# Dividing the first layer's attention sums on VectorE in 32 by 32 pieces instead of through TensorE

## The chip, the cores and the metric

The kernel runs on one core of one Trainium2 chip. The metric is the device time in microseconds of that core; the time of a kernel is the median of several runs. The five engines are written as in the profile: PE is TensorE's matmul, PEld its weight load, DVE is VectorE, ACT is ScalarE, POOL is GpSimd, and SP issues DMAs. All data are float32.

## The reference

Two transformer layers act on x of shape (4, 512, 256), each with gated cross attention to a context of the same shape and a gated feed-forward part. What matters here is the first layer's attention and what surrounds it:

```python
Q = heads(layernorm(x) @ Wq.T + bq)         # 16 heads of 16
K = heads(ctx @ Wk.T + bk)
V = heads(ctx @ Wv.T + bv)
scores = einsum('bhqd,bhkd->bhqk', Q, K) / 4 - 0.1 * |q - k|
attn = softmax(scores)
out = einsum('bhqk,bhkd->bhqd', attn, V)     # back to (b, 512, 256)
x = x + tanh(g_xattn[0]) * (out @ Wo.T + bo)
# feed-forward part of layer 0: weights rounded to -1, 0, 1
x = x + tanh(g_ffn[0]) * (relu(layernorm(x) @ W1q.T + b1) @ W2q.T + b2)
# layer 1: attention with relu on q, k, v and no output matrix, added to x;
# then a mixture of four experts, one per token, with a layernorm behind it
```

## The kernel before, in words

**Groups and slots.** The 16 heads of one batch element are worked in four groups of four heads, (tt, e) with tt = 0, 1 and e = 0, 1; there are 32 groups, 16 for each layer, and group s of layer 0 belongs to batch element s // 4. A group needs four units, one for each block of 128 keys. The main loop goes over these units: `for u in range(-NT, n_units)` (line 1019), 128 of them. One turn of it is called a slot in what follows. In every slot `scores(u, ...)` (line 525) puts out two rounds of matmuls that fill the array by rows of 32: half of a round are the scores whose maxima DVE takes (`maxima`, pm, for unit u + 6), the other half are the scores that ACT turns into exponentials (`weights`, psc, for unit u). DVE drains a slot's four pm banks at line 502, ACT its four psc banks at line 517, and in layer 0 POOL multiplies a part of p by a decay table (line 520).

**What a slot adds.** After the scores `slot(u)` (line 964) emits the rest of that turn. In slots with u % 4 == 0 it is `weighted` (line 538), 32 matmuls that sum a group's weights times values into `po`, which ACT copies to `oT` (line 551). In slots with u % 4 == 2 it is `turned` (line 553): four PE transposes of the maxima (`pmT`) and, for the group before, four PE transposes of oT (`pn`), a reciprocal of the column that holds the sum of weights (`rec`, line 571) and a product (`o`, line 577). After that come jobs from chains: norms, projections of keys and queries (`project`, line 440), values, the feed-forward parts (`ffn0`, line 587), the rounding of the two weight matrices (`quantize`, line 264), and the routing of layer 1.

**What sets their order.** The order on PE, DVE, ACT and POOL is the order in which the program emits instructions; the Tile framework adds the waits. A chain is a list of steps (job, cost, delay), with a first unit, a last unit and chains that must be done before. A slot counts what it has used and takes the job with the earliest due unit among those that may start:

```python
(job, cost, _), last = c["steps"][0]
if last <= u or cost == 0 or used + cost / 2 < SLOT:      # SLOT = 3.1
    can.append((last, len(can), c))
```

`weighted` counts 3.5, `turned` 1.0, and the others what their step says (1.75 for four full matmuls' worth of work).

**Buffers.** All PSUM tiles come from one pool of eight banks that are given out in turn, so each new bank waits until the one given out eight before has been read. xT (input of a projection or of the feed-forward part, transposed) has three places; o has two, oT two, and q four.

**The feed-forward part of layer 0.** `ffn0(b)` begins with `turn_o` (line 591): POOL adds the output bias to x, PE transposes o with eight transposes (`pt_o`) and ACT copies them to `oTT`. Two `product` jobs multiply by Wo; then follow a norm, its transposes, eight `hidden` jobs (`ph`) and two `output` jobs (`py_f`), the first use of the second weight matrix `w2q`. The rounding of a matrix takes a sum, thresholds, four passes `under` on POOL (line 291) and four passes `over` on DVE (line 298).

Of the kernel before, what the change touches and what calls it, by code (L numbers as in the profile page):

```python
# [11 lines left out]
F32 = mybir.dt.float32  # L12
U32 = mybir.dt.uint32
AF = mybir.ActivationFunctionType
ALU = mybir.AluOpType
# [4 lines left out]
P = 128  # L20
B, S, D = 4, 512, 256
H, DK = 16, 16
NT = S // P
# [21 lines left out]
def flamingo_kernel(ctx: ExitStack, tc: tile.TileContext, t: dict, out: bass.AP):  # L45
# [11 lines left out]
    def bank_psum(name):  # L57
        return ps.tile([P, 512], F32, tag="bank", name=name)
# [303 lines left out]
    def transposed(src, dst, name, alone=False):  # L362

        for c in range(NC):
            pt = bank_psum(f"pt_{name}{c}")
            for n in range(NT):
                nc.tensor.transpose(pt[:, ts(n, P)], src[:, n, ts(c, P)], ident)
            (nc.scalar.copy if alone or c == 0 else nc.vector.tensor_copy)(dst[:, c, :], pt)
# [18 lines left out]
    def prepare(layer, b, eng=None, meanwhile=None):  # L387

        nm = f"a{layer}_{b}"
        st = {}  # L390

        def stats():
            st["xn"] = act.tile([P, NT, D], F32, tag="xn", name=f"xn_{nm}")
            first, st["more"], st["rows"] = layernorm(
                x[b], st["xn"], 1e-5, nm, eng, meanwhile
            )
            first()

        def more_stats():
            st["more"]()  # L400

        def norm():
            st["rows"]()

        def turn():
            xTs[layer, b] = act.tile([P, NC, S], F32, tag="xT", name=f"xT_{nm}", bufs=3)
            transposed(st["xn"], xTs[layer, b], nm, layer == 0 and b > 0)

        def values(n0):
            def run():  # L410
                wv = attn_w[layer]["wv"]
                vh = v_sb[b % 2][1]
                pv = bank_psum(f"pv{nm}{n0}")
                for n in range(2):
                    for c in range(NC):
                        nc.tensor.matmul(  # L416
                            pv[:, ts(n, D)], lhsT=cT[b][:, c, ts(n0 + n, P)], rhs=wv[:, c, :],
                            start=(c == 0), stop=(c == NC - 1),
                        )
                if layer == 0:  # L420
                    nc.scalar.copy(
                        vh[:, n0 : n0 + 2, :, 0:DK], pv.rearrange("p (n h d) -> p n h d", n=2, d=DK)
                    )
# [15 lines left out]

    def project(layer, b, tt):  # L440

        nm = f"{layer}_{b}{tt}"

        def product(w, src, name):
            pp = bank_psum(f"{name}{nm}")
            for c in range(NC):
                nc.tensor.matmul(  # L447
                    pp, lhsT=attn_w[layer][w][:, c, ts(tt, P)], rhs=src[:, c, :],
                    start=(c == 0), stop=(c == NC - 1),
                )  # L450
# [12 lines left out]

        def keys(between=None, halves=range(2)):
            pk = product("wk", cT[b], "pk")
            if between:
                between()
            for e in halves:
                key_half(pk, e)

        def queries():
            pq = product("wq", xTs[layer, b], "pq")
            for e in range(2):
                q = act.tile([P, S], F32, tag="q", name=f"q{nm}{e}", bufs=4)
                h = half[:, e : e + 1]
                if layer == 0:
                    nc.scalar.activation(q, pq, AF.Identity, bias=bqk[:, 0, tt, e : e + 1], scale=h)
                elif e == 0:
                    nc.scalar.activation(q, pq, AF.Relu, scale=h)
                else:  # L480
                    nc.vector.tensor_scalar(q, pq, h, 0.0, ALU.mult, ALU.max)
                qs[layer, b, tt, e] = q

        return [(keys, 1.75, 1), (queries, 1.75, 0)]
# [65 lines left out]
        pos[s] = act.tile([P, S], F32, tag="oT", name=f"oT{s}")  # L550
        nc.scalar.copy(pos[s], po)  # L551

    def turned(shifted, divided):


        if shifted is not None:
            g = groups[shifted]
            m = m_sb[g[0]][g[3]]
            pm = bank_psum(f"pmT{shifted}")
            for n in range(NT):  # L560
                nc.tensor.transpose(pm[:, ts(n, P)], m[:, n].rearrange("p h w -> p (h w)"), ident)  # L561
            q2s[g] = act.tile([P, S], F32, tag="q2", name=f"q2_{shifted}")
            nc.vector.tensor_tensor(q2s[g], qs[g], pm, ALU.subtract)
        if divided is not None:
            layer, b, tt, e = groups[divided]
            pn = bank_psum(f"pn{divided}")
            for n in range(NT):
                nc.tensor.transpose(pn[:, ts(n, P)], pos[divided][:, ts(n, P)], ident)  # L568
            pn = pn.rearrange("p (n h w) -> p n h w", h=HG, w=HP)
            rec = sml.tile([P, NT, HG], F32, tag="rec", name=f"rec{divided}")  # L570
            nc.vector.reciprocal(rec, pn[:, :, :, DK])
            if layer == 1:
                nc.vector.tensor_scalar_mul(rec, rec, gx1)
            if (tt, e) == (0, 0):
                os_[layer, b] = act.tile([P, NT, D], F32, tag="o", name=f"o{layer}_{b}")
            ov = os_[layer, b].rearrange("p n (t i e d) -> p n t i e d", t=NC, i=HG, e=2)
            nc.vector.tensor_tensor(  # L577
                ov[:, :, tt, :, e, :], pn[:, :, :, 0:DK],
                rec.unsqueeze(3).to_broadcast([P, NT, HG, DK]), ALU.mult,
            )  # L580
            if layer == 1:
                eng = nc.vector if b >= B - 2 and (tt, e) == (1, 1) else nc.gpsimd
                xv = x[b].rearrange("p n (t i e d) -> p n t i e d", t=NC, i=HG, e=2)[:, :, tt, :, e, :]
                eng.tensor_tensor(xv, xv, ov[:, :, tt, :, e, :], ALU.add)  # L584


    def ffn0(b):

        st = {}

        def turn_o():
            st["oT"] = act.tile([P, NC, S], F32, tag="xT", name=f"oTT{b}", bufs=3)
            nc.gpsimd.tensor_tensor(
                x[b], x[b], bo0.unsqueeze(1).to_broadcast([P, NT, D]), ALU.add
            )
            transposed(os_[0, b], st["oT"], f"o{b}", True)

        def product(n0):
            return lambda: residual(
# [15 lines left out]
            )  # L615

        def turn():
            st["xT"] = act.tile([P, NC, S], F32, tag="xT", name=f"xTf0_{b}", bufs=3)
            transposed(st["xn"], st["xT"], f"f0_{b}")

        def hidden(f):
# [15 lines left out]
        def output(n2):  # L637
# [3 lines left out]

        return (
            [
                (turn_o, 0.9, 0), (product(0), 1.75, 1), (product(2), 1.75, 0), (stats, 0, 1),
                (more_stats, 0, 1),
            ],
            [
# [17 lines left out]
    def route(b, eng=None):  # L665
# [20 lines left out]
            nc.sync.dma_start(out=rd[:, :, D : 2 * D], in_=x[b])  # L686

        def turn():
            st["xT"] = act.tile([P, NC, S], F32, tag="xT", name=f"xTf1_{b}", bufs=3)
            transposed(st["xn"], st["xT"], f"f1_{b}")  # L690

        def products():
# [250 lines left out]
    (totals2, *_), *quant2 = quantize(w2f, "w2")  # L943
    totals = {0: (totals1, 0), 1: (totals1, 2), 2: (totals2, 0), 3: (totals2, 2)}
    quant = chain(quant1, 4, 17)
    chain(quant2, 12, 29, quant)
    chain([(bias_columns, 0, 0), (output_bias, 0.9, 2)], 4, 14)
    fetches = [
        (lambda j=j, f=f: f(j), 0, 0)
# [14 lines left out]
    def slot(u):  # L964
# [3 lines left out]
            used += 3.5  # L968
        if u % NT == 2 and u > 0:
            s = u // NT  # L970
            turned(s + 1 if s + 1 < len(groups) else None, s - 1 if s > 0 else None)
            used += 1.0
        while True:
            can = []
            for c in chains:
# [42 lines left out]
    key_rows(1, 1, nc.gpsimd)  # L1018
    for u in range(-NT, n_units):
        if u == 0:  # L1020
            turned(0, None)
            early_values()
            other_constants()
        if u == 4:
# [85 lines left out]
    hidden_tile(0)  # L1110
    weighted(last)
    turn_tile(1)
    turned(None, last)
    att.__exit__(None, None, None)
    act = ctx.enter_context(tc.tile_pool(name="moe", bufs=2))
    fetch_weights(2)
# [110 lines left out]
```

## Time and profile before

| What | Value |
|---|---|
| Median of 3 runs | 869.88 us (869.17 to 870.01) |
| The profiled execution, its own time | 868.27 us |
| Its span, first to last instruction | 866.0 us |
| Mean granted clock of TensorE | 0.987 |
| PE busy | 836.0 us, 97% of the span |
| DVE busy | 539.2 us, 62% |
| ACT busy | 422.9 us, 49% |
| POOL busy | 271.8 us, 31% |

The slots run from about 15 us to 704 us of the span; the experts of layer 1 take the rest. Slot 16, the first that the change touches, begins at 101.7 us, slot 57 at 328.7 us and slot 101 at 587.7 us. Busy times are sums over an engine's instructions; matmuls are pipelined, and their ends are modelled, so that PE's share counts waits that lie under a running matmul. A group's row gives the line, the engine, the operation, what it writes and reads with the shapes, how often, the busy time, the mean of one in ns, and behind the last bar the engine's idle time before it and who ended that. In a timeline's row the first number is the start, the second the length of the merged run, and in square brackets stands the idle time before it with its releaser.

### The profile page before, as it was taken

The page shows a single profiled execution, that of the slowest core. Times are in us where ns is not written, and L with a number is a line of the kernel's source. Part 1 is how long each engine was busy: PE and PEld are TensorE (multiplying, and loading weights), DVE is VectorE, ACT ScalarE, POOL GpSimd, SP SyncE. Part 2 cuts the span into 40 slices and gives each one's busy share as a digit, 9 for nine tenths or more (in the row PEclk, how much of TensorE's full clock was granted, in tenths as well). Part 3 has the DMA queues.
Part 4 walks back from the last instruction along what each step waited for, and adds up shares of the span by engine and source line. Part 5 has one row for each costly group of instructions (what it writes and reads, how often), then busy time and mean ns, then how long its engine had stood idle before and what let it go on. Part 6 is the DMA issues. An engine that isn't in the chain of part 4 may idle for free.

```text
span 866.0 us, 13669 instructions
## 1 busy us (share of the span) xinstructions
PE 836.0 (97%) x5294; PEld 475.1 (55%) x5294; DVE 539.2 (62%) x1170; ACT 422.9 (49%) x886; POOL 271.8 (31%) x435
## 2 busy tenths in 40 slices
PE   6999999999999999999999999999999999999995
PEld 3444454445464445545446444554444448999994
DVE  6778777665745675467663776567677715644443
ACT  2475565553545563546543664346466563233331
POOL 5536465324242343302100220003002034445542
PEclk9999999999999999999999999999999999999998
DMA  9100000000000000000000010001001046456650
GB/s 314 59 1 1 1 1 2 1 1 1 1 13 25 1 1 1 1 26 1 1 1 1 25 50 1 1 1 50 2 1 48 1 147 215 162 183 201 196 190 15
DMA packets 17776, 42.03 MB, mean 49 GB/s; under 512 B 2158, under 2 KB 12144, under 8 KB 15280
## 3 DMA queue, kind: packets, MB, share of 16 engines
q0 software_dynamic: 5168, 27.08, 9.5%
q1 hardware_dynamic: 12128, 13.54, 4.6%
q8 instruction: 42, 0.69, 0.3%
q10 hardware_dynamic: 416, 0.54, 0.2%
q14 instruction: 22, 0.18, 0.1%
HBM read 34.86 MB, written 6.68 MB: 48 GB/s over the span
## 4 chain that ended last, share of the span: by engine, by line
PE 76%; DVE 7%; issue 6%; POOL 4%; DMA 4%; ACT 2%; POOLq 0%; ACTq 0%; DVEq 0%
PE pm L488 15%; PE po L545 13%; PE psc L488 13%; PE py_f L375 6%; PE ph L625 6%; PE pk L447 4%; PE pva L416 3%; PE pq L447 3%; DVE m L502 3%; DMA out_dram<-y,put 3%; PE pmT L561 2%; PE py_wo L375 2%; PE pn L568 2%; POOL wg L894 2%; POOL out_dram L1102 1%
## 5 line engine op out<-in xcount | busy, mean ns | idle before, releaser
L502 DVE TENSOR_REDUCE m<-pm 128x1 f32<-128x512 f32 x512 | 316.6, 681 | 133.3 <-PE psc L488 130.7
L517 ACT ACTIVATE p<-psc 128x512 f32<-128x512 f32 x512 | 267.2, 603 | 158.0 <-PE psc L488 156.0
L488 PE MATMUL psc<-q,k 32*128 32x512 f32 x1024 | 284.9, 631 | 2.1 <-DVE m L502 1.9
L488 PE MATMUL pm<-k,q 32*128 32x512 f32 x1024 | 266.4, 619 | 2.9 <-DVE m L502 2.0
L520 POOL TENSOR_TENSOR p<-p,dec 128x256 f32<-128x256 f32 x128 | 93.3, 732 | 184.1 <-ACT p L517 184.1
L488 PEld LDWEIGHTS pm<-k,q 32*128 32x128 f32 x1024 | 95.1, 185 | 86.5 <-issue 59.7
L488 PEld LDWEIGHTS psc<-q,k 32*128 32x128 f32 x1024 | 108.6, 185 | 55.8 <-issue 26.5
L545 PE MATMUL po<-p,v 128*32 128x512 f32 x1024 | 117.9, 601 | 1.7 <-DVE m L502 1.6
L1065 ACT ACTIVATE ha<-pg,wg 128x128 f32<-128x128 f32 x152 | 43.2, 369 | 88.6 <-PE pg L1059 83.3
L545 PEld LDWEIGHTS po<-p,v 128*32 128x32 f32 x1024 | 31.6, 110 | 84.5 <-issue 63.3
L1059 PE MATMUL pg<-xs,wg 128*128 128x128 f32 x608 | 71.2, 275 | 0.8 <-DVE xn_f L356 0.8
L1059 PEld LDWEIGHTS pg<-xs,wg 128*128 128x128 f32 x608 | 70.5, 192 | 2.8 <-POOL rstd_f L336 1.2
L1075 PE MATMUL pyf<-wo,ha 128*128 128x256 f32 x304 | 68.6, 379 | 0.0
L584 POOL TENSOR_TENSOR x<-x,o 128x256 f32<-128x256 f32 x14 | 10.2, 730 | 174.0 <-DVE o L577 142.1
L625 PE MATMUL ph<-xTf,w1q 128*128 128x512 f32 x128 | 60.2, 603 | 0.0
L1075 PEld LDWEIGHTS pyf<-wo,ha 128*128 128x128 f32 x304 | 56.4, 190 | 6.9
L551 ACT COPY oT<-po 128x512 f32<-128x512 f32 x32 | 18.7, 585 | 81.4 <-PE po L545 81.4
L375 PE MATMUL py_f<-w2q,h 128*128 128x256 f32 x256 | 57.0, 381 | 0.0
L375 PEld LDWEIGHTS py_f<-w2q,h 128*128 128x128 f32 x256 | 48.0, 190 | 9.2 <-DVE m L502 3.0
L447 PE MATMUL pk<-cT,wk 128*128 128x512 f32 x68 | 35.2, 642 | 7.5 <-DMA cT<-in_ctxT_dram 7.4
L1079 DVE TENSOR_TENSOR y<-y,pyf 128x256 f32<-128x256 f32 x19 | 8.0, 421 | 53.2 <-PE pyf L1075 52.9
L625 PEld LDWEIGHTS ph<-xTf,w1q 128*128 128x128 f32 x128 | 22.4, 190 | 27.7 <-issue 17.2
(197 smaller groups left out, 800.4 us busy)
## 6 DMA issues: line engine op xcount, KB each, us to landing
x<-in_x_dram SPq DMA_DIRECT2D x4, 512.0 KB, 8.6
rows_d<-xn_f SPq DMA_DIRECT2D x4, 512.0 KB, 3.8
rows_d<-x SPq DMA_DIRECT2D x4, 512.0 KB, 3.8
cT<-in_ctxT_dram SPq DMA_DIRECT2D x3, 512.0 KB, 9.5
w1q<-in_w_dram SPq DMA_DIRECT2D x1, 1024.0 KB, 9.1
w2q<-in_w_dram SPq DMA_DIRECT2D x1, 1024.0 KB, 11.3
wo<-in_wo_dram SPq DMA_DIRECT2D x2, 512.0 KB, 3.8
rows<-in_rows_dram SPq DMA_DIRECT2D x1, 640.0 KB, 9.3
```

Of the source, the lines that this page charges most:

```text
L375: nc.tensor.matmul(py[:, n, :], lhsT=operand(c, n0 + n), rhs=w[:, c, :], start=(c == 0), stop=(c == chunks - 1),)
L416: nc.tensor.matmul(pv[:, ts(n, D)], lhsT=cT[b][:, c, ts(n0 + n, P)], rhs=wv[:, c, :], start=(c == 0), stop=(c == NC - 1),)
L447: nc.tensor.matmul(pp, lhsT=attn_w[layer][w][:, c, ts(tt, P)], rhs=src[:, c, :], start=(c == 0), stop=(c == NC - 1),)
L488: nc.tensor.matmul(out_, lhsT=lhs[r, ts(n, P)], rhs=rhs[r, :], start=True, stop=True)
L502: nc.vector.tensor_reduce(m[:, n, 2 * pair + i, r : r + 1], pm[i], AX.X, ALU.max)
L517: nc.scalar.activation(p[:, i, :], psc[i], AF.Exp, scale=SCALE)
L520: nc.gpsimd.tensor_tensor(d, d, dec.unsqueeze(1).to_broadcast([P, 2, P]), ALU.mult)
L545: nc.tensor.matmul(po[i * HP : (i + 1) * HP, :], lhsT=v_sb[b % 2][0][:, kt, c0 : c0 + HP], rhs=ps_exp[NT * s + kt, i // 2][:, i % 2, :], s ...
L625: nc.tensor.matmul(ph, lhsT=w1q[:, c, ts(f, P)], rhs=st["xT"][:, c, :], start=(c == 0), stop=(c == NC - 1),)
L1059: nc.tensor.matmul(ph[:, f, :], lhsT=w[:, c, ts(f2 * NF // 2 + f, P)], rhs=xs[j][:, c, :], start=(c == 0), stop=(c == NC - 1),)
L1065: nc.scalar.activation(ha[:, f, :], ph[:, f, :], AF.Gelu, bias=wg[j][:, NC * FF + fa : NC * FF + fa + 1],)
L1075: nc.tensor.matmul(py, lhsT=hs[j, f // 4][:, f % 4, :], rhs=wo1[f // 4][:, f % 4, :], start=(f == 0), stop=(f == NF - 1),)
```

## The change

`turned` is divided in two functions, `shifted` (the transposes of the maxima, as before) and `divided` (the division as before, for layer 1 and for batch element 0 of layer 0). For batch elements 1 to 3 of layer 0 `divided_blocks` takes its place: DVE transposes oT in 32 by 32 pieces, takes the reciprocals and the products in that layout, and after the second group of a pair transposes both together back, in pieces, straight into the layout that Wo's matmul reads. It is emitted in slots u % 4 == 0, two groups behind, after `weighted`. `turn_o` then has nothing to do for these batch elements, and its bias add is a step of its own. The second half of q in layer 0 is read out of PSUM by DVE for b = 2 and 3. The second matrix's rounding starts at unit 17 (was 12) and is due at 33 (was 29). xT has two places instead of three, and the transposed input of the routing uses the place of `blocks`.

```diff
-            xTs[layer, b] = act.tile([P, NC, S], F32, tag="xT", name=f"xT_{nm}", bufs=3)
+            xTs[layer, b] = act.tile([P, NC, S], F32, tag="xT", name=f"xT_{nm}", bufs=2)
...
-                if layer == 0:
+                if layer == 0 and (e == 0 or b < 2):
                     nc.scalar.activation(q, pq, AF.Identity, bias=bqk[:, 0, tt, e : e + 1], scale=h)
+                elif layer == 0:
+                    nc.vector.tensor_scalar(q, pq, h, bqk[:, 0, tt, e : e + 1], ALU.mult, ALU.add)
...
+    def by_blocks(s):
+        return groups[s][0] == 0 and groups[s][1] > 0
+
+    TB = S // HP
+
+    def divided_blocks(s):
+        layer, b, tt, e = groups[s]
+        if e == 0:
+            blocks[b, tt] = act.tile([P, 2, TB, HP], F32, tag="blocks", name=f"blocks{s}", bufs=1)
+        turn, both = (blocks[b, tt][:, i] for i in range(2))
+        nc.vector.transpose(turn.rearrange("p a w -> p (a w)"), pos[s])
+        rec = sml.tile([P, TB], F32, tag="rec", name=f"rec{s}")
+        nc.vector.reciprocal(rec, turn[:, :, DK])
+        if (tt, e) == (0, 0):
+            os_[layer, b] = act.tile([P, NC, S], F32, tag="o", name=f"o{layer}_{b}")
+        nc.vector.tensor_tensor(
+            both[:, :, e * DK : (e + 1) * DK], turn[:, :, 0:DK],
+            rec.unsqueeze(2).to_broadcast([P, TB, DK]), ALU.mult,
+        )
+        if e == 1:
+            nc.vector.transpose(os_[layer, b][:, tt, :], both.rearrange("p a w -> p (a w)"))
...
-        def turn_o():
-            st["oT"] = act.tile([P, NC, S], F32, tag="xT", name=f"oTT{b}", bufs=3)
+        def output_biases():
             nc.gpsimd.tensor_tensor(
                 x[b], x[b], bo0.unsqueeze(1).to_broadcast([P, NT, D]), ALU.add
             )
-            transposed(os_[0, b], st["oT"], f"o{b}", True)
+
+        def turn_o():
+            st["oT"] = os_[0, b]
+            if b == 0:
+                st["oT"] = act.tile([P, NC, S], F32, tag="xT", name=f"oTT{b}", bufs=2)
+                transposed(os_[0, b], st["oT"], f"o{b}", True)
...
-                (turn_o, 0.9, 0), (product(0), 1.75, 1), (product(2), 1.75, 0), (stats, 0, 1),
+                (output_biases, 0, 0), (turn_o, 0 if b else 0.9, 0), (product(0), 1.75, 1 + int(b > 0)),
+                (product(2), 1.75, 0), (stats, 0, 1),
...
-            st["xT"] = act.tile([P, NC, S], F32, tag="xT", name=f"xTf1_{b}", bufs=3)
+            st["xT"] = act.tile([P, NC, S], F32, tag="blocks", name=f"xTf1_{b}", bufs=1)
...
-    chain(quant2, 12, 29, quant)
+    chain(quant2, 17, 33, quant)
...
-            turned(s + 1 if s + 1 < len(groups) else None, s - 1 if s > 0 else None)
-            used += 1.0
+            if s + 1 < len(groups):
+                shifted(s + 1)
+                used += 0.5
+            if s > 0 and not by_blocks(s - 1):
+                divided(s - 1)
+                used += 0.5
+        if u % NT == 0 and u >= 2 * NT and by_blocks(u // NT - 2):
+            divided_blocks(u // NT - 2)
```

More of the change, by code (lines that the diff above doesn't have):

```diff
@@ L551, in weighted @@
         nc.scalar.copy(pos[s], po)
[L553 to L584, printed above, removed]
@@ new lines, in shifted @@
+    def shifted(s):
+        g = groups[s]
+        m = m_sb[g[0]][g[3]]
+        pm = bank_psum(f"pmT{s}")
+        for n in range(NT):
+            nc.tensor.transpose(pm[:, ts(n, P)], m[:, n].rearrange("p h w -> p (h w)"), ident)
+        q2s[g] = act.tile([P, S], F32, tag="q2", name=f"q2_{s}")
+        nc.vector.tensor_tensor(q2s[g], qs[g], pm, ALU.subtract)
+    def by_blocks(s):
[17 more added lines that the diff above has]
+            nc.vector.transpose(os_[layer, b][:, tt, :], both.rearrange("p a w -> p (a w)"))
@@ new lines, in flamingo_kernel, with divided @@
+    blocks = {}
+    def divided(s):
+        layer, b, tt, e = groups[s]
+        pn = bank_psum(f"pn{s}")
+        for n in range(NT):
+            nc.tensor.transpose(pn[:, ts(n, P)], pos[s][:, ts(n, P)], ident)
+        pn = pn.rearrange("p (n h w) -> p n h w", h=HG, w=HP)
+        rec = sml.tile([P, NT, HG], F32, tag="rec", name=f"rec{s}")
+        nc.vector.reciprocal(rec, pn[:, :, :, DK])
+        if layer == 1:
+            nc.vector.tensor_scalar_mul(rec, rec, gx1)
+        if (tt, e) == (0, 0):
+            os_[layer, b] = act.tile([P, NT, D], F32, tag="o", name=f"o{layer}_{b}")
+        ov = os_[layer, b].rearrange("p n (t i e d) -> p n t i e d", t=NC, i=HG, e=2)
+        ov = ov[:, :, tt, :, e, :]
+        nc.vector.tensor_tensor(
+            ov, pn[:, :, :, 0:DK], rec.unsqueeze(3).to_broadcast([P, NT, HG, DK]), ALU.mult
+        )
+        if layer == 0:
+            return
+        eng = nc.vector if b >= B - 2 and (tt, e) == (1, 1) else nc.gpsimd
+        xv = x[b].rearrange("p n (t i e d) -> p n t i e d", t=NC, i=HG, e=2)[:, :, tt, :, e, :]
+        eng.tensor_tensor(xv, xv, ov, ALU.add)
@@ L617, in turn @@
         def turn():
-            st["xT"] = act.tile([P, NC, S], F32, tag="xT", name=f"xTf0_{b}", bufs=3)
+            st["xT"] = act.tile([P, NC, S], F32, tag="xT", name=f"xTf0_{b}", bufs=2)
             transposed(st["xn"], st["xT"], f"f0_{b}")
@@ L1020, in flamingo_kernel @@
         if u == 0:
-            turned(0, None)
+            shifted(0)
             early_values()
@@ L1112, in flamingo_kernel @@
     turn_tile(1)
-    turned(None, last)
+    divided(last)
     att.__exit__(None, None, None)
```

## The prediction

> **What bounds the kernel now.** I read the page first (busy shares, then the slices), then the groups of instructions kept apart by shape, then the timeline slot by slot, then the list of waits. "Slot" is one turn u of the main loop: two rounds of scores on PE, then the jobs that `slot(u)` adds; in the timeline it begins where pm and psc start again after other PE work.
>
> The page: the span, the engines, and the slices of PE and DVE.
> ```profile
> span 866.0 us, 13669 instructions
> ...
> PE 836.0 (97%) x5294; PEld 475.1 (55%) x5294; DVE 539.2 (62%) x1170; ACT 422.9 (49%) x886; POOL 271.8 (31%) x435
> ...
> PE   6999999999999999999999999999999999999995
> ...
> DVE  6778777665745675467663776567677715644443
> ```
> PE is full in nearly every slice; DVE, which takes the work over, is at five to seven tenths. But a busy PE may be a PE that waits on a buffer, so the slots must be read one by one.
>
> Three stretches in the view by windows: PE's slot 38 (one product after pmT and pn), slot 44 (the 32 matmuls of `weighted`), slot 99 (scores alone). Columns: length, then busy time and count of PE, PEld, DVE, ACT, POOL.
> ```profile
> 222.70:227.52 4.82, 4.82 (x34) 3.06 (x33) 3.68 (x8) 2.93 (x6) 2.17 (x3) 1.00 0.00 0
> ...
> 257.92:263.49 5.57, 5.57 (x50) 1.94 (x49) 3.17 (x5) 2.90 (x6) 3.22 (x5) 1.00 0.21 49
> ...
> 578.03:580.68 2.65, 2.12 (x17) 0.84 (x16) 2.37 (x8) 1.73 (x4) 0.73 (x1) 1.00 0.00 0
> ```
> With jobs in it a slot is as long as PE's work: 5.57 us full, 4.82 us with one product. Without jobs (2.65 us) it is as long as DVE's four maxima, 2.48 us. So work taken off PE is worth its time only where the slot keeps enough other PE work.
>
> **The change, part by part.** The groups by shape that I cost with:
> ```profile
> L502 DVE TENSOR_REDUCE m<-pm 128x1 f32<-128x512 f32 x512 | 316.6, 681 | 133.3 <-PE psc L488 130.7 <-PE pm L488 2.6
> ...
> L568 PE MATMUL pn<-ident,oT 128*128 128x128 f32 x128 | 20.6, 284 | 0.3 <-ACT oT L551 0.3
> ...
> L577 DVE TENSOR_TENSOR o<-pn,rec 128x256 f32<-128x256 f32 x32 | 13.6, 424 | 1.1
> ...
> L571 DVE RECIPROCAL rec<-pn 128x16 f32<-128x16 f32 x32 | 7.9, 248 | 8.7 <-PE pn L568 8.7
> ...
> L368 DVE COPY xTf<-pt_f 128x512 f32<-128x512 f32 x8 | 5.5, 683 | 1.2 <-PE pt_f L367 1.2
> ...
> L367 PE MATMUL pt_o<-ident,o 128*128 128x128 f32 x32 | 4.5, 281 | 0.5 <-DVE m L502 0.5
> ```
> (1) The pn transposes of groups 4 to 15 go. Their means (284 ns) overlap; the cost on PE is the pitch, read in slot 38:
> ```profile
> 224.67 0.66 PE L561 MATMUL pmT<-ident,m 128*128 128x128 f32 x4
> 225.20 0.66 PE L568 MATMUL pn<-ident,oT 128*128 128x128 f32 x4
> 225.70 1.89 PE L375 MATMUL py_wo<-wo,oTT 128*128 128x256 f32 x8
> ```
> From pn's start to the product's is 0.50 us. The product inherits the PSUM bank that pn had, and that was free at 225.20, so it can start there: 12 x 0.50 = -6.0 us, in slots 22, 26, ... 66.
>
> (2) The eight transposes of `turn_o` go for b = 1 to 3, slots 35, 51, 67. In slot 51 pt_o starts at 298.82 and the next work at 299.75: 0.93 each, -2.8 us. The ACT copies behind them (600 ns, six) lie beside PE.
>
> (3) rec and o leave the slots u%4 == 2. In slots 34 and 50 DVE's queue ran over: in slot 51 the round psc of 297.77 waited for a bank that DVE's h freed at 297.71, behind rec and o and a norm's statistics. PE's own work in a slot is the sum of its pitches (a round of four 512-column tiles 0.41, a full 512-column matmul 0.43, 256 columns 0.216, a transpose 0.11); slots 35 and 51 are 1.39 us longer than that, most others 0.5 to 0.6. With 0.25 + 0.42 us taken away (0.65 by the starts), -0.65 in each: -1.3 us.
>
> (4) DVE's new work: for each of 12 groups a 32x32 transpose of 128x512, a reciprocal and a product, for each odd one a second transpose. No row shows the transpose. The Trainium skill ("VectorE: DVE Perf Modes", section "The three transpose paths") gives 311 ns for 128 columns of bf16; my rows of 512 and 256 columns (683 and 418 ns) differ by 265 ns, so 384 more columns add 0.40: an estimate of 0.71 us, next to the 0.683 of the copy of the same shape. Low end 0.53 (512 columns at 265/256 ns, no fixed part), high end 1.37, twice the copy, if four-byte elements take two beats. I take 0.71. Then an even group costs 0.71 + 0.25 + 0.42 + gaps = 1.43 us, an odd one 2.2 us. The same page's table for kernel authors speaks against the change: a full 128x128 transpose belongs on TensorE. By summed engine time it is right, 0.50 us of PE against 0.71 or 1.42 of DVE, and if DVE were the bound the change would lose 18 x 0.71 = 12.8 us. What decides is where the work lies: in slots u%4 == 0, behind the maxima and beside the 3.6 us of po. DVE in slot 44 and into 45:
> ```profile
> 259.08 2.48 DVE L502 TENSOR_REDUCE m<-pm 128x1 f32<-128x512 f32 x4 [0.36 <-PE psc L488]
> 264.65 0.69 DVE L502 TENSOR_REDUCE m<-pm 128x1 f32<-128x512 f32 x1 [3.08 <-PE psc L488]
> ```
> DVE is idle for 3.08 us there; 2.2 fits. In slots 24, 40 and 56 the FFN's statistics come behind the blocks, but slot 40 still leaves 2.67 us idle after them (next maxima at 240.50) and the group is even, 1.43. Nothing waits inside the chain: oT was copied four slots earlier. I take +0.3 us for jitter. Without the cover each group would cost up to 2.2 us.
>
> Contention: o's product now has two SBUF inputs, and POOL multiplies p by dec meanwhile (732 ns). The skill ("SBUF — State Buffer", section "Who interferes with whom") says such an instruction contends with a GpSimd one that reads SBUF, and that one fully blocks. The row nearest to it, L298 with w and neg, runs at 718 ns at best and at 1088 median for w1q, with POOL's neg beside it: +0.37. By the rule up to 12 x 0.73 = 8.8 us of DVE time, by the row 4.4; both inside the idle 0.9 us left, so 0 on the path.
>
> (5) q's second half moves to DVE for b = 2, 3, four times. The two readers of a bank go one after the other in layer 1 also, and the next slot's psc waits for pq's bank:
> ```profile
> DVE q L481 <- ACT q L479: 5.9, 6, 1.5
> ...
> 234.72 0.29 PEld L488 LDWEIGHTS psc<-q,k 32*128 32x128 f32 x2 [0.44 <-ACT q L477]
> ```
> ACT, ACT is 773 + 773; ACT, DVE 773 + 0.05 + 751: no gain, and the maxima behind it start up to 0.5 us later. Slots 40 and 24 are 1.32 over PE's work, their likes 56 and 72 in layer 1, where DVE has the half, 1.50 and 1.49. +0.1 each, +0.4 us.
>
> (6) The second rounding moves: total, limits, four unders (POOL, 1.56 each) and four overs (DVE, 0.77) run in slots 17 to 27 instead of 16 to 26. Its PE part is one 128x1 matmul; SP has nothing. Slots 20, 22, 24 and 26 lose a DVE job, 21, 23, 25, 27 gain one; w2q is first read in slot 35 either way. 0, bounds -0.5 (slot 20's wait eases) and +0.7 (slot 23: keys, statistics, q and over together fill DVE). The bias add on POOL (2.37 us) now comes ahead of the next norm's deviations in slots 35, 51, 67; POOL's sum per slot is as before and the norm's rows on ACT start only after oT's copy, a slot later: 0.
>
> (7) Fewer places for xT: taken through the order of jobs, the tightest reuse is slot 26, where xTf0 takes the place that slot 22's product read last. No wait, 0; were one such reuse to wait for a hidden product, 1.7 us.
>
> (8) The planner. A job may start while used + cost/2 < 3.1; turned cost 1.0, shifted costs 0.5, turn_o 0. A u%4 == 2 slot still takes one product of 1.75 (0.5 + 1.75 + 0.9 is over 3.1), so slots get shorter, not fuller, there. But slots 35, 51, 67 take more, and jobs of layer 0's FFN then move up: output(0) of b = 1 from slot 58 to 57, of b = 2 from 78 to 74, of b = 3 from 94 to 91, its output(2) from 97 to 94. The other slots are permuted at one price. Slot 97 (9.03 us now) is left with scores, and 98 with shifted, divided and statistics. There DVE sets the length: slot 97 about 2.4 instead of PE's 2.1, +0.3; slot 98 like slot 10 (4.65 us, with turned alone and as much DVE work, 5.2) instead of 4.82 - 1.72 = 3.1, +1.55. Together +1.9 us. After slot 100 the order is the old one.
>
> Sum: -6.0 - 2.8 - 1.3 + 0.3 + 0.4 + 1.9 = -7.5 us. The profiled execution took 868.27 (span 866.0 and 2.3 around it), so 860.8 there; the median shown is 1.6 higher, 869.88, and I forecast 862.4.
>
> **The rivals.** A, DVE takes back half: each added DVE job shifts maxima somewhere, PE waits on banks. For it: weight loads already stand idle until "DVE m" for 23.4 us (pmT), 13.7 (pm), 12.8 (po), 10.5 (ph) and 10.3 (pk) in the list of waits, a part of which is real; and the L298 spread. Against: the 3.08 us. With (3) worth nothing, +1 us in slots 23 to 25, 39 to 41 and 55 to 57 and 0.3 in each odd group: -7.5 + 1.3 + 3 + 1.8 = -1.4, 868.5; half of that -4, 866.
>
> B, no gain: pn and pt_o filled waits. If the product after pmT could not start before the old time for lack of its bank, (1) and (2) are void and +1.3 remains, offset by (3): about 870. Against: slot 38's bank was free.
>
> C, slower: the DVE transpose is the bound. Place: odd groups' slots, 28, 36, ... 68. Over 3.08 us the rest delays the maxima, and PE waits for banks: 6 x (2T + 0.7 - 3.08). It eats the 7.5 at T = 1.8 us. At T = 2.73, four beats per element, it is 6 x 3.08 = 18.5, and even groups add 3 x 0.35 + 3 x 0.76 = 3.3: +14.3, 884. For it: no row of a DVE transpose. Against: a page's 311 ns has no room for four beats unless the element's size sets them.
>
> **How the numbers follow.** This kernel's runs differ by 0.1%, so about 0.2%, 1.7 us, can be told from no change. Forecast (859 to 865.5): 0.62. A: 0.18, nearly all below 868.1. B: 0.06. C and its milder forms: 0.14. Faster 0.80, same 0.06, slower 0.14. The low end, 858.5, has (8) at nothing and (6) at its gain, and overlaps some more; the high end, 870.0, takes in T = 1.37 (6 x 0.36 = 2.2) on top of A, and B. What is left out is C and a thin lower tail.
>
> **What would show it.** Right: slots 22 to 66 with u%4 == 2 about 4.3 us; slots 36, 44, 52 still near 5.57; DVE's transpose row near 0.7; slot 98 longer than 3.1; maxima in slots 29, 45, 53 starting about 1.16 us after the slot. Wrong: po slots over 5.8 us, a transpose row over 1.3, weight loads that wait for DVE's o or blocks, a span that shrinks by under 4 us.

## The result, and the profile after

The changed kernel takes 864.76 us (median of four runs, 862.88 to 865.25), the kernel before beside it 869.94 (869.17 to 870.95, four runs): 5.2 us less, ratio 0.9936, 95% interval 0.9918 to 0.9954. A later run of the same kernel gave 865.11. The forecast was 862.4. The profiled execution took 865.25 us, 3.0 less than that of before. Lines have shifted: scores are now L490, maxima L504, `weighted` L547, the pn transposes of the remaining groups L598.

The page of the changed kernel: span, engines, the slices of DVE, and the granted clock.
```profile
span 863.2 us, 13527 instructions
...
PE 832.9 (96%) x5222; PEld 472.6 (55%) x5222; DVE 555.2 (64%) x1192; ACT 418.2 (48%) x876; POOL 271.7 (31%) x435
...
DVE  6778778766857784768646865577777615644443
...
PEclk9999999999999999999999999999999799999998
```
DVE works 16 us more than before, and PE is still busy for 96% of the span. One thing in it is not of the change: the 7 in slice 32 of the clock. I come back to it.

The stretch in which every edit lies, from the start of slot 16 to the start of slot 100, in the view by windows (length, then busy time and count of PE, PEld, DVE, ACT, POOL, then the granted clock, DMA share, GB/s). First before, then after, with slots 38 and 44 of after below it.
```profile
102.32:581.29 478.97, 476.62 (x2931) 240.25 (x2929) 306.52 (x577) 245.82 (x466) 129.82 (x199) 1.00 0.02 7
```
```profile
102.19:574.57 472.38, 470.67 (x2860) 234.34 (x2858) 322.25 (x599) 241.20 (x456) 129.40 (x199) 1.00 0.02 7
...
219.63:224.05 4.42, 4.42 (x29) 2.67 (x28) 3.13 (x6) 2.92 (x6) 2.16 (x3) 1.00 0.00 0
254.24:259.81 5.57, 5.57 (x50) 1.93 (x49) 5.00 (x9) 2.90 (x6) 3.21 (x5) 1.00 0.18 51
```
The clock is at full rate here in both, so this is the cleanest measure of the change: 478.97 to 472.38, -6.6 us. Slot 38 went from 4.82 to 4.42 us. Slot 44 kept its 5.57 us to the hundredth, with DVE at 5.00 us in it instead of 3.17: the new work lies under `weighted`.

The groups by shape that answer to those of before.
```profile
L504 DVE TENSOR_REDUCE m<-pm 128x1 f32<-128x512 f32 x512 | 316.6, 682 | 106.3 <-PE psc L490 103.5 <-PE pm L490 2.6
...
L598 PE MATMUL pn<-ident,oT 128*128 128x128 f32 x80 | 12.9, 285 | 0.3 <-ACT oT L553 0.3
...
L578 DVE STREAM_TRANSPOSE blocks<-oT 128x512 f32<-128x512 f32 x12 | 8.4, 701 | 0.0
...
L583 DVE TENSOR_TENSOR blocks<-blocks,rec 128x256 f32<-128x256 f32 x12 | 5.3, 441 | 0.4
...
L588 DVE STREAM_TRANSPOSE o<-blocks 128x512 f32<-128x512 f32 x6 | 4.3, 711 | 0.2
...
L479 DVE TENSOR_SCALAR q<-pq,cols,bqk 128x512 f32<-128x512 f32 x4 | 3.2, 810 | 2.3 <-ACT q L477 2.2
L580 DVE RECIPROCAL rec<-blocks 128x16 f32<-128x16 f32 x12 | 3.0, 254 | 0.4
...
L367 PE MATMUL pt_o<-ident,o 128*128 128x128 f32 x8 | 1.1, 280 | 0.0
```
The unknown of the forecast, the DVE transpose of 128x512 four-byte elements, is 701 and 711 ns against an estimate of 710. 48 pn transposes and 24 of pt_o are gone. The maxima wait 106.3 us for PE instead of 133.3: the idle time of DVE has been spent.

DVE in slot 44 and into 45 (start, length, instruction, and in brackets the idle time before it with its releaser).
```profile
255.40 2.48 DVE L504 TENSOR_REDUCE m<-pm 128x1 f32<-128x512 f32 x4 [0.36 <-PE psc L490]
257.80 0.70 DVE L578 STREAM_TRANSPOSE blocks<-oT 128x512 f32<-128x512 f32 x1
258.54 0.25 DVE L580 RECIPROCAL rec<-blocks 128x16 f32<-128x16 f32 x1
258.83 0.42 DVE L583 TENSOR_TENSOR blocks<-blocks,rec 128x256 f32<-128x256 f32 x1
259.29 0.71 DVE L588 STREAM_TRANSPOSE o<-blocks 128x512 f32<-128x512 f32 x1
260.97 1.29 DVE L504 TENSOR_REDUCE m<-pm 128x1 f32<-128x512 f32 x2 [0.97 <-PE psc L490]
```
This is an odd group, the longer kind. It runs from 257.80 to 260.00, in what was a gap of 3.08 us, and leaves 0.97 us of it. The maxima of slot 45 start 1.16 us after the slot (259.81), as forecast: nothing was delayed.

### The profile page after: what moved, and what is told of

Same layout as the page of the kernel before. It is cut to its first block, busy times and chain, and to the rows that moved or that the text cites. A ratio compares the mean times of both kernels' runs of the same rounds, so it can differ in the third digit from the quotient of the medians.

```text
span 863.2 us, 13527 instructions
## 1 busy us (share of the span) xinstructions
PE 832.9 (96%) x5222; PEld 472.6 (55%) x5222; DVE 555.2 (64%) x1192; ACT 418.2 (48%) x876; POOL 271.7 (31%) x435
## 4 chain that ended last, share of the span: by engine, by line
PE 74%; DVE 9%; issue 8%; POOL 5%; DMA 2%; ACT 1%; POOLq 0%; ACTq 0%; DVEq 0%
PE pm L490 15%; PE po L547 13%; PE psc L490 13%; PE ph L660 7%; PE py_f L375 7%; PE pk L447 4%; PE pva L416 4%; DVE m L504 4%; PE pq L447 3%; PE pmT L561 2%; PE py_wo L375 2%; DMA out_dram<-y,put 2%; POOL out_dram L1144 2%; POOL wg L930 2%; POOL rstd_y L1132 1%
## 5 line engine op out<-in xcount | busy, mean ns | idle before, releaser
L504 DVE TENSOR_REDUCE m<-pm 128x1 f32<-128x512 f32 x512 | 316.6, 682 | 106.3 <-PE psc L490 103.5
L490 PE MATMUL psc<-q,k 32*128 32x512 f32 x1024 | 286.6, 635 | 2.1 <-DVE m L504 1.9
L490 PE MATMUL pm<-k,q 32*128 32x512 f32 x1024 | 266.8, 618 | 2.6 <-DVE m L504 1.7
L490 PEld LDWEIGHTS pm<-k,q 32*128 32x128 f32 x1024 | 95.7, 185 | 87.7 <-issue 51.4
L490 PEld LDWEIGHTS psc<-q,k 32*128 32x128 f32 x1024 | 108.6, 186 | 55.5 <-issue 25.2
L547 PE MATMUL po<-p,v 128*32 128x512 f32 x1024 | 117.0, 597 | 1.9 <-DVE m L504 1.9
L547 PEld LDWEIGHTS po<-p,v 128*32 128x32 f32 x1024 | 31.8, 110 | 83.5 <-issue 62.6
```

The source lines that it names most:

```text
L490: nc.tensor.matmul(out_, lhsT=lhs[r, ts(n, P)], rhs=rhs[r, :], start=True, stop=True)
L504: nc.vector.tensor_reduce(m[:, n, 2 * pair + i, r : r + 1], pm[i], AX.X, ALU.max)
L547: nc.tensor.matmul(po[i * HP : (i + 1) * HP, :], lhsT=v_sb[b % 2][0][:, kt, c0 : c0 + HP], rhs=ps_exp[NT * s + kt, i // 2][:, i % 2, :], s ...
```

## The experiments

Each experiment is an edit of the changed kernel, except one that edits the kernel before. Ratios are to runs of the kernel before beside it, whose medians were 869.75, 869.78 and 869.47 in the three groups of runs. Because single runs scatter by 1 to 4 us with the granted clock (under "The clock"), I set beside each median the length of the clean stretch, slot 16 to slot 100, where the change has 472.4.

**The same kernel again**, to see what repeats.

> The changed kernel once more, as the base of the three beside it, on the same chip: 864.8 (862.9 to 865.3).

865.11 us, 0.9951 (0.9933 to 0.9969); clean stretch 472.40. The stretch repeats to 0.02 us although the clock's dips fall elsewhere. It can therefore tell apart edits that the medians cannot.

**Is the gain PE's time?** Unread transposes give PE back what the change took away (their banks take a turn in the pool, too); DVE keeps its new work. `turn_o` gets, in the same way, eight transposes of cT[b] into two banks for b > 0.
```diff
+            if s > 0 and by_blocks(s - 1):
+                idle = bank_psum(f"idle{s}")
+                for n in range(NT):
+                    nc.tensor.transpose(idle[:, ts(n, P)], pos[s - 1][:, ts(n, P)], ident)
```


> The changed kernel with TensorE's removed work put back as matmuls that nobody reads: four transposes of oT in the slots u%4 == 2 of the 12 groups, and eight transposes of the context for b = 1 to 3 where turn_o had them. Theory (the gain is TensorE's time alone): 12 x 0.40 + 3 x 0.97 = +7.7 us, 872.5, some 2.5 over the kernel before, since the planner's order and q cost something. Rival (the gain is that rec and o left these slots on VectorE): 865 to 867.

871.24 us, 1.0017 (1.0007 to 1.0028).
```profile
99.92:578.78 478.86, 477.10 (x2932) 241.38 (x2927) 322.88 (x599) 241.65 (x457) 129.52 (x199) 1.00 0.02 7
...
199.48:209.67 10.19, 10.19 (x57) 7.85 (x57) 4.61 (x11) 2.06 (x4) 6.23 (x11) 1.00 0.00 0
```
The clean stretch is back at 478.86, +6.5 us, where 7.7 was expected. The twelve slots of pn give back 4.9 us, all that the change had gained there, so rival B (the transposes only filled waits) is out for them. The slots of pt_o (35, 51, 67) give back 0.43, 0.45 and 0.96 us of the 0.97 expected for each. Slot 35, the second row, holds the same jobs in all three kernels: 10.81 us before, 10.19 here, 9.76 in the change. So 0.62 us of its gain stays with PE's work back, and that part is what rec and o leaving DVE is worth there. Most of the gain is thus PE's pitch, but not all of it. That the whole stretch comes within 0.1 us of before's 478.97 is chance in so far: what slots 35 and 51 and the later rounding keep is used up by q and the planner (the edits undone below).

**How much DVE time lies free?** The block transpose is done twice, or (with range(4)) four times, into the same tile; the repeats change nothing that is read.
```diff
-        nc.vector.transpose(turn.rearrange("p a w -> p (a w)"), pos[s])
+        for _ in range(2):
+            nc.vector.transpose(turn.rearrange("p a w -> p (a w)"), pos[s])
```


> The changed kernel with one more VectorE transpose of oT into the same place in each of the 12 groups by blocks, 12 x 0.70 = 8.4 us of VectorE work. Theory (cover): an odd group then needs 2.85 us of the 3.08 that were idle, an even one 2.15 of 2.67 or more, so the time stays at 864.8, at most 1 us more. Rival A (each VectorE job in these slots shifts maxima and costs about half of itself): 869.

> Three more transposes in each of the 12 groups, 25 us of VectorE work. Theory (cover with an edge): odd groups overrun their 3.08 us by 1.2, even ones their 2.67 to 3.08 by 0.5 to 0.9, together 7.2 + 4.2 = 11.4 us if the overrun passes wholly to TensorE: 870 to 876. Rival A (proportional): three times what one more transpose cost, 877. No effect at all (865) would say that VectorE has no part in the pace of these slots.

One more: 863.31 us, 0.9923 (0.9907 to 0.9940). In the clean stretch DVE is busy 8.5 us longer (330.76 against 322.25), and the stretch is 472.40, as long as the change's within 0.02 us. Three more: 875.88 us, 1.0065 (1.0046 to 1.0084).
```profile
101.76:585.79 484.03, 471.50 (x2860) 234.23 (x2856) 346.50 (x635) 241.97 (x457) 129.15 (x199) 1.00 0.02 7
```
24.3 us more DVE work cost 11.65 us, nearly the forecast. DVE with three more in slots 44 and 45, then PE in slot 45:
```profile
263.18 2.94 DVE L579 STREAM_TRANSPOSE blocks<-oT 128x512 f32<-128x512 f32 x4
...
266.90 0.71 DVE L589 STREAM_TRANSPOSE o<-blocks 128x512 f32<-128x512 f32 x1
267.54 2.44 DVE L504 TENSOR_REDUCE m<-pm 128x1 f32<-128x512 f32 x4
```
```profile
268.24 1.98 PE L447 MATMUL pk<-cT,wk 128*128 128x512 f32 x4 [1.06 <-DVE m L504]
```
Slot 45 begins at 265.18 here, so its maxima start 2.36 us in, not 1.16; PE then waits 1.06 us for a bank, and the slot takes 6.69 us, not 5.56. That is rival C's mechanism, made on purpose. One transpose of cover, 0.7 us a group, is left unused in the change, three are not.

**Does the place matter?** The same DVE work, called in the slot where rec and o used to be (u%4 == 2) instead of beside `weighted`.
```diff
-            if s > 0 and not by_blocks(s - 1):
+            if s > 0 and by_blocks(s - 1):
+                divided_blocks(s - 1)
+            elif s > 0:
                 divided(s - 1)
-        if u % NT == 0 and u >= 2 * NT and by_blocks(u // NT - 2):
-            divided_blocks(u // NT - 2)
```


> The changed kernel with the division by blocks back in the slots u%4 == 2, one group behind, where the old division stood. Theory (the place is the cover): these slots are 4.43 us long, and their maxima, q2, the blocks and the residual end 0.9 (even) to 1.6 us (odd) after the next slot's maxima are ready; 12 groups x 0.5 to 1 us: 871 to 877, the gain is gone. Rival (the place does not matter, only TensorE's work does): 865.

876.82 us, 1.0078 (1.0058 to 1.0097): slower than before by 7 us.
```profile
101.60:588.82 487.22, 478.31 (x2860) 236.38 (x2855) 321.65 (x599) 242.50 (x457) 128.93 (x199) 1.00 0.02 7
```
The instructions are those of the change, and the stretch is 14.8 us longer, of which a dip of the clock, the only one in any of these stretches, accounts for up to 1.7: half rate for 3.41 us in slot 35, behind a wait of 1.68 us. DVE in slots 38 and 39 (slot 39 starts at 231.14):
```profile
230.87 0.70 DVE L578 STREAM_TRANSPOSE blocks<-oT 128x512 f32<-128x512 f32 x1
231.61 0.25 DVE L580 RECIPROCAL rec<-blocks 128x16 f32<-128x16 f32 x1
231.90 0.42 DVE L583 TENSOR_TENSOR blocks<-blocks,rec 128x256 f32<-128x256 f32 x1
232.24 0.74 DVE L380 SCALAR_TENSOR_TENSOR x<-py_wo,tg,x 128x512 f32<-128x512 f32 x1
232.90 2.47 DVE L504 TENSOR_REDUCE m<-pm 128x1 f32<-128x512 f32 x4
```
An even group, and still DVE's queue is without a gap and the maxima start 1.76 us into the slot. Behind even groups, slots 23, 39 and 55 became 1.0 us longer (6.58 against 5.60 in 39) and slot 63 1.4. Behind odd groups, slots 27, 51 and 67 became 1.7 to 2.3 us longer and slot 43 0.6; slot 35 took 13.51 us (9.76 in the change), the dip included. Slots 31, 47 and 59 lost nothing. So the moved place of the blocks is not a detail of the change: at the old place the trade loses.

**The other edits, each undone alone**: q wholly on ACT in layer 0; the second rounding at its old time; the planner's old costs, which bring back the old order of jobs (beside the line of the diff, `used += 0.5` for every s > 0, not only where `divided(s - 1)` is called).
```diff
-                if layer == 0 and (e == 0 or b < 2):
+                if layer == 0:
...
-    chain(quant2, 17, 33, quant)
+    chain(quant2, 12, 29, quant)
...
-                (output_biases, 0, 0), (turn_o, 0 if b else 0.9, 0), (product(0), 1.75, 1 + int(b > 0)),
+                (output_biases, 0, 0), (turn_o, 0.9, 0), (product(0), 1.75, 1 + int(b > 0)),
```


> The changed kernel with q's second half of layer 0 on ScalarE for all batch elements, as before. Theory: the two readers of a bank go one after the other in any case, and in the changed kernel's slots 24, 30, 40, 46 some 0.17 us each are lost: 0.7 us faster than the changed kernel, 864.1. Rival (two engines empty the bank sooner): slower by 0.5 to 1.

860.15 us, 0.9889 (0.9871 to 0.9908). The windows of the stretch and of slots 24 and 40 with q on ACT, then slots 24 and 40 of the change:
```profile
101.64:573.03 471.39, 469.91 (x2860) 233.79 (x2855) 319.37 (x595) 243.41 (x461) 128.91 (x199) 1.00 0.02 7
140.14:146.37 6.23, 6.23 (x50) 1.94 (x49) 6.03 (x16) 3.39 (x6) 1.47 (x2) 1.00 0.00 0
229.06:235.29 6.23, 6.23 (x49) 1.94 (x48) 5.61 (x15) 3.39 (x6) 1.52 (x3) 1.00 0.01 3
```
```profile
140.07:146.78 6.71, 6.48 (x50) 2.15 (x49) 6.50 (x16) 2.95 (x5) 1.46 (x2) 1.00 0.00 0
229.65:236.06 6.41, 6.41 (x50) 1.95 (x49) 6.16 (x16) 2.95 (x5) 1.46 (x2) 1.00 0.01 3
```
q's half on DVE costs 0.48 and 0.18 us in these slots and 0.18 each in slots 30 and 46, 1.0 us in all (472.38 to 471.39). The median fell by 5 us against the change, and the trace shows the reason for 1.0 of them. Over the runs of all kernels the time falls by about 0.6 us for each 0.001 of mean granted clock; by that, about 1.3 us are dips of the clock that these four runs were spared (mean clock 0.9875, against 0.985 over the ten runs of the change). The other 2 to 3 are not settled.

> The changed kernel with the second matrix rounded from unit 12, due at 29, as before. Theory: slots 16 to 27 gained 0.4 us beside the transposes, so 0.4 us slower, 865.2, hardly to be told from no change. Rival (the move was needed because the rounding and the blocks meet in slot 24): 1 to 2 us slower.

866.13 us, 0.9960 (0.9948 to 0.9972); stretch 473.41, +1.0 us. Slot 27 of this kernel by windows, and DVE in it:
```profile
154.91:162.13 7.22, 7.15 (x25) 2.92 (x25) 4.88 (x7) 4.26 (x8) 4.56 (x5) 1.00 0.00 0
```
```profile
155.29 1.51 DVE L298 SCALAR_TENSOR_TENSOR w2q<-w2q,qthr_w,neg_w 128x512 f32<-128x512 f32 x1
156.72 0.68 DVE L368 COPY xTf<-pt_f 128x512 f32<-128x512 f32 x1
157.32 2.47 DVE L504 TENSOR_REDUCE m<-pm 128x1 f32<-128x512 f32 x4
```
The rounding step, at twice its median of 0.74 us, stands ahead of the maxima, which start 2.41 us into the slot. In the change it comes behind them and takes 0.74 us; the maxima start 1.16 us in, and slot 27 takes 6.03 us. In the kernel before, that step took up to 0.88 us and slot 27 6.73. Against before, the slots of the rounding (17 to 20, 23, 27) sum to -0.8 us; against this kernel it is -1.0. The forecast had put the edit at nothing, with bounds of -0.5 and +0.7.

> The changed kernel with the planner's old costs (1.0 in slots u%4 == 2, 0.9 for turn_o), so that all jobs stand in the slots of the kernel before and the division alone is changed. Theory: slots 97 to 99, which were left with 1.4 us more than TensorE's work, keep their jobs: 1.4 us faster than the changed kernel, 863.4. Rival (the moved jobs only changed places): the same, 864.8.

864.67 us, 0.9940 (0.9923 to 0.9958). Stretch 471.81: the new order of jobs costs 0.6 us net. The medians can't tell this kernel or the one before it from the change. With the old jobs in their old slots, slots 51 and 67 can be set against before directly: 5.61 to 4.56 us and 4.81 to 3.85. But slot 68 then grows from 5.53 to 6.18 us, which it does not in the change (5.50).

**The clock.** In the profiled run of the change, 3.4 of the microseconds gained were lost again in slots 122 and 123, which no edit touches. Slots 122 and 123 by windows: before, then after.
```profile
682.12:693.70 11.58, 9.71 (x53) 6.01 (x49) 9.19 (x29) 5.65 (x11) 0.73 (x1) 0.85 0.01 1
```
```profile
675.25:690.23 14.98, 13.11 (x52) 8.45 (x49) 9.35 (x29) 5.66 (x11) 0.73 (x1) 0.65 0.00 1
```
The same work and the same waits, at a granted clock of 0.85 and 0.65. PE in the change, where the dip begins:
```profile
674.88 1.98 PE L490 MATMUL psc<-q,k 32*128 32x512 f32 x5
678.73 2.43 PE L490 MATMUL psc<-q,k 32*128 32x512 f32 x4 [1.87 <-DVE m L504]
...
685.01 5.29 PE L881 MATMUL pid_d<-tid_d,sel_d 128*128 128x9 f32 x24
```
PE stood idle for 1.87 us behind DVE, and the clock was at half from 679.60 to 693.25; the 24 small matmuls took 5.29 us, which take 2.85 at full clock. Before has the same wait of 1.87 us but only two dips of 3.41 us each near it (from 687.21 and 694.04). The starts of the dips in one trace lie whole multiples of 3.41 us apart (in before also 28.44 and 656.49), and this grid lies differently against the kernel in each run. To test this I gave PE something to do ahead of the two waits of that kind: 24 transposes of an old tile into a bank that nobody reads, after the jobs of slots 115 and 121, in the change and in the kernel before.
```diff
+        if u in (115, 121):
+            for i in range(24):
+                idle = bank_psum(f"warm{u}_{i}") if i == 0 else idle
+                nc.tensor.transpose(idle[:, ts(i % NT, P)], cT[3][:, 0, ts(i % NT, P)], ident)
```


> The changed kernel with 24 transposes that nobody reads (2.6 us of TensorE) behind slots 115 and 121, ahead of the two places late in layer 1 where TensorE waits for the routing on VectorE and its granted clock falls to 0.5. Theory (clock): the waits shrink, fewer windows at half clock follow in slots 122 to 124, 1 to 2 us faster in the median, 863, and the runs lie closer together. Rival (those slots are VectorE's order alone): up to 5.2 us slower, 865 to 870.

> The kernel before with the same 2 x 24 idle transposes. If the clock there blurs the comparison alike in both kernels, this one moves as the changed kernel does under them, 868 to 869, and the gap between the two is the 6.6 us that the slots 16 to 100 show. Rival: the changed kernel alone is hit by the clock, and this one does not move.

The change with it: 860.69 us, 0.9903 (0.9883 to 0.9923). Before with it: 866.11, 0.9967 (0.9952 to 0.9983). More work on PE, and both became faster, by 4 and 3 us. Slots 122 and 123 of the change with the idle transposes:
```profile
677.65:685.34 7.69, 7.69 (x50) 5.09 (x49) 6.54 (x16) 4.43 (x8) 0.73 (x1) 1.00 0.01 2
```
7.69 us at full clock. A part of that is only shifted: slot 121 now holds PE's filler and takes 4.86 us instead of 1.95, during which DVE catches up, so slots 121 to 123 come to 12.55 us against 16.93 (13.53 in the repeat of the change, which had fewer dips). Between these two kernels the change is worth 5.4 us by the medians, as between the two without filler (5.2): in the medians, the dips at these waits raise both alike.

**The undone edits together, and with the filler.** q on ACT and old costs; then that with the idle transposes.

> The changed kernel with both small undoings: q's halves all on ScalarE, and the planner's old costs. In slots 16 to 100 the one gave 1.0 and the other 0.6 us: 1.6 us faster than the changed kernel there, a median of 863; if the 4 us by which the first one's median moved are real, 859 to 860.

> The same with the 2 x 24 idle transposes: 1 to 2 us faster than without them, 858 to 862, if the clock theory holds; 2 to 5 slower if it does not.

859.60 us, 0.9889 (0.9869 to 0.9909), with a clean stretch of 470.81, that is 1.57 less than the change and just the 0.99 and 0.57 of the two edits. With the filler 858.57 us, 0.9878 (0.9856 to 0.9901). This is the fastest version run, 10.9 us under the kernel before, though its interval overlaps that without the filler. Its profiled run, 856.07 us, had a mean clock of 0.997; that of the version without filler, 864.24 us, had 0.984.

## Why the prediction was right, and where it was off

The mechanism was right: work taken off PE is worth its pitch where PE sets the slot, and DVE's new work is free beside `weighted`. All eight steps lie in the clean stretch, where they sum to -7.5 and measured -6.6. The median came out 2.4 us above the forecast.

| step | forecast | measured | read from |
|---|---|---|---|
| (1) pn | -6.0 | -4.9 | twelve slots, -0.39 in most (30 and 46 with q on ACT, -0.44) |
| (2) pt_o and (3) backlog | -4.1 | -3.1 | slots 35, 51, 67 at equal jobs: -1.05, -1.05, -0.97 |
| (4) DVE's blocks | +0.3 | 0.0 | slots 28, 36, 44, 52 unchanged to 0.01 us |
| (5) q's half | +0.4 | +1.0 | slots 24, 40, 30, 46; q on ACT |
| (6) rounding later | 0 | -0.8 to -1.0 | its slots; rounding at its old time |
| (7) places of xT | 0 | no wait seen | the waits |
| (8) planner | +1.9 | +1.4 in its slots, +0.6 net | slots 97 to 99; old costs |

With (8) at +1.4 the measured terms sum to -6.4 to -6.6: the stretch is accounted for.

(1) The term was 12 x 0.50. PE in slot 38 of the change:
```profile
221.59 0.66 PE L561 MATMUL pmT<-ident,m 128*128 128x128 f32 x4
222.13 2.00 PE L375 MATMUL py_wo<-wo,o 128*128 128x256 f32 x8
224.05 0.70 PE L490 MATMUL pm<-k,q 32*128 32x512 f32 x2
```
The product starts 0.54 us after pmT instead of 1.03, so its start moved by 0.49 as said. But from there to the next slot it is 1.92 us, where it was 1.82 (225.70 to 227.52). That tenth in each slot is the miss. The product's weight loads in slot 38, before and after:
```profile
225.59 1.60 PEld L375 LDWEIGHTS py_wo<-wo,oTT 128*128 128x128 f32 x8
```
```profile
222.13 1.59 PEld L375 LDWEIGHTS py_wo<-wo,o 128*128 128x128 f32 x8
```
Before, the first load starts 0.11 us ahead of the product, under pn. In the change it starts with the product, whose second matmul follows its first after 0.32 us instead of 0.22.

(3) is the step that failed most: the forecast took 0.65 us off the wait in each of slots 35 and 51, and the wait shrank by 0.22. In slot 35 DVE's h frees the bank. Here it is before, with PE's work put back, and in the change:
```profile
202.61 0.72 DVE L633 TENSOR_SCALAR h<-ph,b 128x512 f32<-128x512 f32 x1
```
```profile
199.91 0.72 DVE L673 TENSOR_SCALAR h<-ph,b 128x512 f32<-128x512 f32 x1
```
```profile
200.37 0.72 DVE L668 TENSOR_SCALAR h<-ph,b 128x512 f32<-128x512 f32 x1
```
The slot starts at 201.56, 199.48 and 199.54, so h ends 1.77, 1.15 and 1.55 us into it (in slot 51 1.76, 1.15 and 1.54). Without rec and o, DVE reaches h 0.62 us sooner against PE, nearly as forecast; with PE's work put back, that shows. But (1) had made slot 34 0.40 us shorter, so in the change PE, too, comes to the wait sooner, and only 0.22 is left (0.93 for pt_o and 0.22, less a tenth as in (1), is the 1.05 measured). The forecast counted the same time in (1) and in (3). The norm's statistics still stand ahead of h, so the wait stays.

(5) was priced by likeness to layer 1. In slots 24 and 40 DVE's q stands directly ahead of the maxima, and in slot 24 a rounding step besides; it took 810 ns, not 751.

(6) was called neutral because each slot that gains a step is paired with one that loses it. The slots were not alike: the early place puts a slow step ahead of the maxima in slot 27, the late place puts it behind them.

(8) is near in its sum, but not in its slots, and that is partly luck: slot 98 took 3.88 us, not 4.65, slot 97 1.90, not 2.4, and slot 99, which the forecast left alone, 3.45 instead of 2.65. The step from +1.4 to +0.6 net is mostly slot 68. With the old jobs slot 67 is only 3.85 us long, DVE comes into slot 68 with statistics and h still to do, and the wait for h's bank costs 0.65 us there. In the change slot 67 holds four more matmuls, and that wait is gone.

Contention: the forecast had POOL at work beside every one of the twelve products, and took from the row 0.37 us for each, and more from the Trainium skill ("SBUF — State Buffer", section "Who interferes with whom"). In the change ten of the products had no POOL instruction beside them and one had 23 ns of one; these took 424 to 427 ns. The one with POOL at work beside it took 617 ns (612 in the repeat). That agrees with the page, but it is one product, and three steps of the second rounding took 741 to 744 ns with POOL beside them, the last step with the early rounding 1.51 us. That contention cost nothing on the path is due to POOL's idle time, which the forecast had not looked for.

The rule that a full transpose belongs on TensorE ("VectorE: DVE Perf Modes", section "Rules for kernel authors") holds by summed time, 0.50 us against 0.70, and decides at the old place (+14.8 us in the stretch); at the new place the idle engine's dearer transpose won.

What the forecast did not have is the clock. In the profiled pair it is the main reason why -6.6 us in the stretch became -3.0: 3.4 us were lost in slots 122 and 123. From slot 127 to the end the change took 0.9 us more, which is not explained. How the medians come to -5.2 is not taken apart like that. With filler in both kernels the gap is still 5.4, and there the profiled run of the change has a dip in slot 124 and one in the experts' stage (at 686.3 and 754.6 us), that of before only one (703.7); but medians have no trace.

Two of the signs named for a wrong forecast came up. The span shrank by 2.8 us, under 4; the stretch and the dips of the clock say why. And weight loads wait for DVE's blocks in the list of waits:
```profile
PEld pm L490 <- DVE blocks L583: 7.5, 9, 0.8
```
But a weight load's idle time is not PE's: in slot 45 the load stands idle for 0.84 us in both kernels, under the matmuls of po, and slot 44 kept its length. DVE's transpose row (0.70), slots 36, 44 and 52 and slot 98 came out as the forecast's own signs had them.

Rival A had DVE take back half; the shortfall of (5), 0.6 us, is of that kind. That of (2) and (3), 1.0 us, is not: the queue there is the old one. Rival C needed a transpose of 1.8 us; it is 0.70.

What stays open, beside that: why the median with q on ACT fell by 5 us, of which the trace shows 1.0. No experiment moved the norm's statistics that still stand ahead of h in slots 35 and 51.

## What to carry to other kernels

Moving work to a slower engine pays where that engine waits anyway; measure the gap (3.08 us here), fit the chain into it (2.2 us), and put it behind the instruction that others wait for, since the same chain at the old place, two slots earlier, turned a gain of 5 us into a loss of 7. Do not add two gains at one wait: a change that frees a bank 0.62 us sooner, and also brings PE to that bank 0.40 us sooner, shortens the wait by 0.22 only. When removed work is put back as a test, a slot that grows by all of it was set by that work; one that grows by half had been waiting. Where medians differ by less than the scatter, compare a stretch at full clock: it repeated here to 0.02 us.

## What the runs showed of the hardware

- The granted clock halves for a fixed time, 3.41 us or a multiple (13.65 us in the change), near points where TensorE had waited: 1.87 us behind DVE in slot 122, 1.68 us in slot 35 with the blocks at their old place. Not every wait is followed by a dip: slots 51 and 67 of that kernel have waits of 1.68 and 1.62 us and none, and the dip at 694.04 in before has no wait over 0.4 us close ahead of it. The dips of one trace lie on a grid of 3.41 us. Where they fall differs from run to run of the same kernel, and with them the time by 1 to 4 us. 48 idle transposes ahead of two such waits made the change 4 us and the kernel before 3 us faster.
- A VectorE transpose in 32x32 pieces of 128x512 four-byte elements takes 0.70 us, close to the copy of that shape out of PSUM (0.68), and four in a row 2.94.
- Four TensorE transposes taken from between two other groups of matmuls gave back 0.39 us of their 0.50; the next group's first weight load had run under them.
